# RMS-norm sums in four column tiles with inverses through DRAM, and three moves of work around them, in an attention and convolution kernel

## The chip, the cores and the metric

The kernel runs on one core of one Trainium2 chip. The metric is the device time of one launch in microseconds (us). All arithmetic is in fp32. One profiled execution gives the durations; its span is the time between the first and the last instruction that the profiler records.

## The reference

The input `x` has 4 images of 1024 channels and 32 x 32 positions, so N = 1024 tokens an image. Layer 0 is attention with 16 heads of 64, layer 1 a bottleneck block of convolutions. Cut to what matters:

```python
# layer 0, per image, h = x as tokens (N x 1024)
qkv = h @ w_qkv.T + b_qkv
q, k = apply_rope(q, cos, sin), apply_rope(k, cos, sin)
q, k = rmsnorm(q, q_norm_w), rmsnorm(k, k_norm_w)       # over all 1024 channels of a token
attn = softmax(q @ k.T * hd ** -0.5)                     # per head
out = rmsnorm((attn @ v) @ w_proj.T, norm_out_w) + h     # v * rsqrt(mean(v * v) + eps) * w
# layer 1, on the 4 images together
y = relu(bn(conv1x1(out, w1)))                           # 1024 -> 256 channels, bn over batch and positions
y = relu(bn(conv3x3(y, w2)))                             # 256 -> 256
y = bn(conv1x1(y, w3))                                   # 256 -> 1024
return relu(out + softplus(residual_scale) * y)
```

So each image has three RMS norms (of q, of k, of the output projection y), twelve in all. Each needs, for every token, a sum of squares over 1024 channels and then 1 / sqrt of it.

## The kernel before, in words

**Layout.** Channels lie on the 128 partitions (8 blocks, `NT`), tokens along the free dimension (two halves of `CH` = 512). The four projections Q, K, V and Y (the output projection) of an image are made with block products of the Strassen and Winograd kind: Q, V and Y of images 1 to 3 with two levels (`project2`), the others with one (`project`). The operands of such products are sums and differences of blocks, made by VectorE (L448 to L452 within `project2`), and the products are added up by VectorE (`add`, L466) after ScalarE has copied the first of each out of PSUM (L527 and its neighbours). V is made with tokens on the partitions (`tokens`). Seven outer products make a projection; `outer_done` finishes blocks of the result.

**Order of the work.** The images run one after the other: Q, K, V, attention, Y. TensorE's list is the program's order. Work of other engines is placed among the products by hand: `product_done(share)` is called after products and advances a counter by units (one unit is four fp32 matmuls of 512 columns; TensorE needs 3.45 us for it). `after(n, step)` puts a step n units later, on the list `later`; `waiting` is a queue of steps with costs, of which one is taken whenever the account `room` is positive, and `spend(cost)` charges the account. A cost of `TT` = 0.21 stands for one VectorE operation of 128 x 512. The engines execute their own lists in order, so a VectorE instruction that waits holds up all that is behind it.

**The norms.** While a projection's blocks are finished, ScalarE squares them and VectorE adds the squares over the 8 channel blocks into `total` (128 x 1024; tiles `sqq`, `sqk`, `sqy`). `inverse_rms` then sums over the partitions: for each half one matmul with a 128 x 128 matrix of ones (`ss`, L650), which leaves every partition with the sum; ScalarE takes the root (L651), and a unit later VectorE the reciprocal (L656), 128 x 512 each. The function `then` that comes after differs: for q and k, `rope` multiplies the cosine and sine tables by the inverses (`tables`, L666 and L667), then for each of 8 channel blocks makes two products (`turn`, L673) and adds one into the other, with neighbouring partitions swapped, through two accumulating DMAs on POOL's queue (L679). For y, `o_norm` multiplies y by the inverses (L790), adds the residual x by an accumulating DMA from DRAM (L791) and stores the result to DRAM as `x1d` (L792), both on POOL's queue. It does so for whole channel blocks, but for the last image in 16 halves.

**Attention** goes through 2 token halves `c` and 8 head pairs `hp`. A head pair has 32 matmuls `sc` (L732) for the scores, the exponential on ScalarE (L739), 32 matmuls `cx` (L749) for the product with V, sums of the probabilities on VectorE (`den`, L741 and L743), and a copy of `cx` by ScalarE (L754). After every second pair four matmuls of 32 columns of ones (`dn`, L768) sum the denominators of four heads into four quarters of the partitions of one PSUM bank, and VectorE takes reciprocals (L774), which SP's DMAs spread (L782). `extra` is a list of steps of which one is run in each pair, used by images 0 and 1 only for preparing weights.

**The last image and layer 1.** In the last image's Y, `queue_filters` loads the raw 3x3 filters (nine loads `t_w<-in_w_dram` on SP) and queues five steps in `waiting` that make the sums of the Winograd filters (L857, L859, L860 on VectorE and one multiplication by ScalarE each; three steps on 128 x 512, two on 128 x 1024). The 1x1 convolution (`c`, L809) of images 1 and 2 comes after Y, reading `back`, which SP loads from `x1d`; that of image 3 reads y directly. Batch statistics, the pads (L1013, L1023) and the 3x3 convolution (`c2x`, `c2y`, L1095) follow.

Of the kernel before, what the change touches and what calls it, by code (L numbers as in the profile page):

```python
# [11 lines left out]
F32 = mybir.dt.float32  # L12
# [6 lines left out]
P = 128  # L19
# [66 lines left out]
def program(ctx, tc, x, wblk, w2, w3, vecs, cos, sin, out, bad):  # L86
# [59 lines left out]

    wd2 = dram.tile([3, len(OUTER), len(SUMS), P, CH], F32, name=f"wd2{u}")
    dens = dram.tile([P, CH], F32, name=f"dens{u}")


    with tc.tile_pool(name=f"st{u}", bufs=2) as st, ExitStack() as s:
# [37 lines left out]
        def bank(kind, name):  # L189
            pool, shape = psum[kind]  # L190
            return pool.tile(shape, F32, tag=kind, name=name)

        def temp(name):
            return tmp.tile([P, CH], F32, tag="tmp", name=name)
# [42 lines left out]

        TT = 0.21
        later, waiting = [], deque()
        pace = {"at": 0, "room": 0.0}  # L240

        def spend(cost):
            pace["room"] -= cost
# [1 line left out]
        def after(n, step):  # L245
            later.append((pace["at"] + n, step))

        def product_done(share=1.0):
            pace["at"] += share
            pace["room"] = min(pace["room"] + share, 1.2)  # L250
            due = [s for at, s in later if at <= pace["at"]]
            later[:] = [(at, s) for at, s in later if at > pace["at"]]
            for step in due:
                step()
            while waiting and pace["room"] > 0:
                next_waiting()

        def next_waiting():
# [154 lines left out]
        def project2(b, which, base, right, room, spare, dest, tokens, tag, ready):  # L413
# [97 lines left out]
            second(0)  # L511
            for k in range(len(OUTER)):
                more = k + 1 < len(OUTER)
                o = banks_[k][0]
                mm(o, w[k][2], t_[k][1], False, False)
                nc.scalar.copy(part(k, 0, 1), o)
                product_done(H2)
                ob = banks_[k][2] = bank2("o2", f"p5_{n}_{k}")
                mm(ob, w[k][3], t_[k][0], True, False)
                p5 = temp(f"p5_{n}_{k}").rearrange("p (q e) -> p q e", q=2)  # L520
                nc.scalar.copy(p5, ob)
                product_done(H2)
                if more:
                    start(k + 1)
                    inner(k + 1, 0)
                mm(o, w[k][4], t_[k][2], False, False)
                nc.scalar.copy(part(k, 1, 1), o)  # L527
                after(2 * H2, lambda k=k, p5=p5: add_to(k, 1, 1, p5))
                product_done(H2)
                if more:  # L530
                    second(k + 1)
                    inner(k + 1, 1)
                mm(ob, w[k][5], b_(k, 1, 1), False, True)
                after(2 * H2, lambda k=k, ob=ob: add_to(k, 0, 1, ob))
                product_done(H2)
                mm(o, w[k][6], t_[k][3], False, True)
                if k > 4:
                    after(2 * H2, lambda k=k, o=o: add(target(k, 1, 0), target(k, 1, 0), o))
                else:
                    nc.scalar.copy(part(k, 1, 0), o)  # L540
                after(2 * H2, lambda k=k: outer_done(k))
                product_done(H2)

        def qk_proj(b, base, bs, ts, bias, dst, tag, w1=None, two=None):

# [94 lines left out]

            return operand(bs, ts), room, spare

        def inverse_rms(total, eps, scale, name, then, lag=4):

            def root():
                for c in range(NCH):
                    o = bank("o2", f"ss_{name}_{c}")
                    nc.tensor.matmul(o, ones, total[:, half[c]], start=True, stop=True)  # L650
                    nc.scalar.activation(total[:, half[c]], o, AF.Sqrt, bias=eps, scale=scale)  # L651
                after(1, invert)

            def invert():
                for c in range(NCH):
                    waiting.append((5 * TT, lambda c=c: nc.vector.reciprocal(total[:, half[c]], total[:, half[c]])))  # L656
                    then(c)

            after(lag, root)

        def rope(b, dst, total, eps, scale, w, tag, rc, biased=True):

            def tables():
                nc.vector.tensor_tensor(rc, cosT, total, ALU.mult)  # L666
                nc.vector.tensor_tensor(total, sinT, total, ALU.mult)  # L667

            def turn(f):
                k, other = dst[:, f, :], big_temp(f"{tag}s_{b}_{f}")  # L670
                for i, (t, table) in enumerate(((other, total), (k, rc))):
                    if w is not None:
                        nc.vector.scalar_tensor_tensor(t, k, w[i][:, f : f + 1], table, ALU.mult, ALU.mult)  # L673
                    elif biased:
                        nc.vector.tensor_tensor(t, k, table, ALU.mult)
                    else:
                        nc.vector.scalar_tensor_tensor(t, k, col("bq", f), table, ALU.add, ALU.mult)
                for i in range(2):
                    nc.gpsimd.dma_start(dst[i::2, f, :], other[1 - i :: 2, :], accum_op=ALU.add)  # L679

            def then(c):
                if c == 0:
                    return
                waiting.append((4 * TT, tables))
                for f in range(NT):
                    waiting.append((4 * TT, lambda f=f: turn(f)))

            inverse_rms(total, eps, scale, f"{tag}_{b}", then)
# [93 lines left out]
                    nc.sync.dma_start(w[j * QH : (j + 1) * QH, half[i]], r[q, :])  # L782
                ready.append((c, hp - 1 + i, w[:, half[i]]))

        def o_norm(b, total, ys, last):


            def norm(f, at):
                y = ys[:, f, at]
                nc.vector.scalar_tensor_tensor(y, y, col("ow", f), total[:, at], ALU.mult, ALU.mult)  # L790
                nc.gpsimd.dma_start(y, x[b, f * P : (f + 1) * P, at], accum_op=ALU.add)  # L791
                nc.gpsimd.dma_start(x1d[f, :, b * N + at.start : b * N + at.stop], y)  # L792

            def then(c):
                if last:
                    waiting.extend([(TT, lambda f=f: norm(f, half[c])) for f in range(NT)])
                elif c == 1:
                    waiting.extend([(2 * TT, lambda f=f: norm(f, slice(0, N))) for f in range(NT)])

            inverse_rms(total, eps_rms, 1.0 / C, f"y_{b}", then, 5 if last else 4)  # L800

        def conv1_weights(name):
            return [[block(W1, f, ih, f"c1_{name}_{f}_{ih}") for ih in range(2)] for f in range(NPT)]
# [38 lines left out]

        uw = {}

        def queue_filters():
            raw = t_tiles("w2")
            taps = w2.rearrange("p (c k f) -> p c k f", c=NPT, k=9)
            for dy in range(3):
                for dx, slot in enumerate((0, 1, 3)):
                    nc.sync.dma_start(  # L850
                        raw[dy][:, slot, :].rearrange("p (c f) -> p c f", c=NPT), taps[:, :, 3 * dy + dx, :]
                    )
            two = [tp.tile([P, 2, CH], F32, tag=n, name=f"u2_{n}") for n in ("cos", "sin")]

            def sums_of(g0, g1, g2, new):

                nc.vector.tensor_tensor(new, g0, g2, ALU.add)  # L857
                nc.scalar.mul(g1, g1, 0.5)
                nc.vector.scalar_tensor_tensor(g1, new, 0.5, g1, ALU.mult, ALU.add)  # L859
                nc.vector.tensor_tensor(new, new, g1, ALU.subtract)  # L860

            for dy in range(3):
                r = raw[dy]
                waiting.append((3 * TT, lambda r=r: sums_of(r[:, 0], r[:, 1], r[:, 3], r[:, 2])))
            for h in range(2):
                js = slice(2 * h, 2 * h + 2)
                waiting.append(
                    (6 * TT, lambda h=h, js=js: sums_of(*(raw[dy][:, js] for dy in range(3)), two[h]))
                )
            for i in range(4):  # L870
                for j in range(4):
                    uw[i, j] = two[j // 2][:, j % 2] if i == 2 else raw[(0, 1, None, 2)[i]][:, j]

        def read_back(b, rows=range(NT)):
            for i in rows:
# [29 lines left out]
        for b in range(B):  # L905
# [31 lines left out]
                    made.append(prepare(*todo.pop(0), pieces))  # L937

            extra = [extra_step] * (len(todo) + 1) if todo else []
            late, ready = [], []  # L940
            probs_ = xp.tile([P, N // P, 2, CH], F32, tag="x", name=f"p_{b}")
            for c in range(NCH):
# [34 lines left out]
                        after(5 * (k - 3) + 0.5, lambda k=k: after(4, prepare(1, WV, k, big_pieces)))  # L977
            else:
                back = {B - 3: x_tile(b + 1)}
                after(3, queue_filters)  # L980
                for i in range(NT):
                    after(8 + 1.5 * i, lambda i=i: read_back(B - 3, (i,)))
            yt[b] = kp.tile([P, NT, N], F32, tag="k", name=f"y_{b}")
            two = (2, *in_place(q_all, tc_, yt[b], False)) if b > 0 else None
            ty = qk_proj(b, WP, q_all, tc_, None, yt[b], "y", None, two)
            o_norm(b, ty, yt[b], b == B - 1)

        back[B - 2] = kv.tile([P, NT, N], F32, tag="q", name="back")
        read_back(B - 2)
        w = conv1_weights("last")  # L990
        for b in (B - 3, B - 2):
            for c in range(NCH):
                for f in range(NPT):
                    conv1(b, f, c, w, back[b])
# [335 lines left out]
```

## Time and profile before

| | |
|---|---|
| time, median of 3 runs | 2788.1 us (2787.07 to 2788.9) |
| profiled execution, its own time | 2789.47 us |
| its span | 2787.7 us |
| mean granted TensorE clock | 0.994 |
| TensorE busy | 2741.8 us, 98% of the span |
| VectorE busy | 2001.5 us, 72% |
| ScalarE busy | 1040.6 us, 37% |
| POOL busy | 375.7 us, 13% |
| gaps over 0.5 us in TensorE's list | 30.4 us together |

Engines are written PE (TensorE), DVE (VectorE), ACT (ScalarE), POOL and SP, the last two mostly issuing DMAs. A line of the timeline has the start and the length in us, engine, line, operation, output and inputs by the tiles' names, shapes and the number of instructions run together; in square brackets the idle time of the engine before it and what it waited for. PE shows two records for each fp32 matmul. Busy time is an average over stages: what a change is worth is read at the place where it acts.

### The profile page before, as it was taken

Reading aid. Unit: us, or ns where it says so; the run is one execution under the profiler, and the core shown is the slowest. Engines: PE = TensorE matmul, PEld = TensorE weight load, DVE = VectorE, ACT = ScalarE, POOL = GpSimd, SP = SyncE. Lnnn points to the kernel's source line nnn. Section 1 sums busy time; section 2 is a strip of 40 time slices with the busy share of each in tenths; the row PEclk is TensorE's granted clock in tenths of the full one; section 3 lists DMA queues with packets and bytes.
Section 4 is the critical chain, followed back from the end, with each engine's and each line's share of the span. In section 5 each row is a group of like instructions: output and inputs, shape, how many; then the busy total and the mean of one; then the engine's idle time right before and its main releaser. Section 6 shows DMA issues by size and latency. Waiting matters only on the chain.

```text
span 2787.7 us, 31160 instructions
## 1 busy us (share of the span) xinstructions
PE 2741.8 (98%) x11194; PEld 1568.1 (56%) x11194; DVE 2001.5 (72%) x2209; ACT 1040.6 (37%) x1419; POOL 375.7 (13%) x427
## 2 busy tenths in 40 slices
PE   9999999999999999999999999999999999998997
PEld 4449533348647533488558333687476333855853
DVE  4356599767727898888748777887567777855987
ACT  1221455323222455433322555333223554322266
POOL 1022022121100121101101001101101001011000
PEclk9999999999999999999999999999999999999999
DMA  5366254277645551267647100558555101664165
GB/s 204 98 170 163 85 165 141 82 257 209 178 111 156 141 160 55 58 204 227 160 126 191 35 17 16 166 148 260 136 152 151 24 16 43 188 203 126 62 213 210
DMA packets 211171, 383.90 MB, mean 138 GB/s; under 512 B 24369, under 2 KB 96561, under 8 KB 211009
## 3 DMA queue, kind: packets, MB, share of 16 engines
q1 hardware_dynamic: 178400, 275.85, 31.7%
q0 software_dynamic: 32608, 105.97, 15.7%
q8 instruction: 91, 1.49, 0.2%
q14 instruction: 72, 0.58, 0.1%
HBM read 254.59 MB, written 76.81 MB: 119 GB/s over the span
## 4 chain that ended last, share of the span: by engine, by line
PE 93%; DMA 3%; DVE 2%; ACT 1%; issue 0%; POOL 0%; SPq 0%; DVEq 0%; ACTq 0%; POOLq 0%
PE sc L732 16%; PE cx L749 16%; PE p_v L434 9%; PE p_q L439 8%; PE p_y L439 8%; PE pa_k L295 8%; PE pc_k L295 4%; PE c L1234 4%; PE c L809 2%; PE pa_q L295 2%; PE pa_v L303 2%; PE pa_y L295 2%; PE pb_k L295 2%; PE c2x L1095 2%; PE c2y L1095 2%; DMA y<-in_x_dram 1%
## 5 line engine op out<-in xcount | busy, mean ns | idle before, releaser
L743 DVE TENSOR_TENSOR den<-den,p 128x1024 f32<-128x1024 f32 x384 | 470.5, 1225 | 41.1 <-DVE den L741 0.5
L739 ACT ACTIVATE p<-sc 128x1024 f32<-128x1024 f32 x512 | 476.6, 1043 | 59.9 <-PE sc L732 59.9
L732 PE MATMUL sc<-q,k 64*128 64x512 f32 x2048 | 460.9, 600 | 8.8 <-DVE v L466 7.4
L749 PE MATMUL cx<-p,v 128*64 128x512 f32 x2048 | 453.6, 595 | 0.0
L732 PEld LDWEIGHTS sc<-q,k 64*128 64x128 f32 x2048 | 192.3, 187 | 275.2 <-issue 125.0
L749 PEld LDWEIGHTS cx<-p,v 128*64 128x64 f32 x2048 | 141.4, 137 | 304.3 <-issue 304.3
L713 POOL TENSOR_SCALAR q<-q,vec 128x512 f32<-128x512 f32 x64 | 123.6, 1939 | 676.8 <-DVE q L712 676.8
L754 ACT COPY q<-cx 128x512 f32<-128x512 f32 x64 | 37.5, 586 | 357.5 <-PE cx L749 357.5
L439 PE MATMUL p_y<-q,w_y 128*128 128x256 f32 x696 | 159.3, 383 | 4.1 <-DVE q L449 4.1
L741 DVE TENSOR_TENSOR den<-p 128x1024 f32<-128x1024 f32 x64 | 76.6, 1196 | 120.1 <-ACT p L739 120.1
L434 PE MATMUL p_v<-w_v,x 128*128 128x256 f32 x696 | 157.1, 379 | 0.0
L439 PE MATMUL p_q<-to,w_q 128*128 128x256 f32 x672 | 152.3, 380 | 0.0
L439 PEld LDWEIGHTS p_y<-q,w_y 128*128 128x128 f32 x696 | 132.9, 192 | 25.7 <-DVE q L449 5.0
L434 PEld LDWEIGHTS p_v<-w_v,x 128*128 128x128 f32 x696 | 132.2, 190 | 19.3 <-issue 1.4
L439 PEld LDWEIGHTS p_q<-to,w_q 128*128 128x128 f32 x672 | 128.0, 191 | 19.1 <-issue 1.8
L774 DVE RECIPROCAL rec<-dn 128x512 f32<-128x512 f32 x32 | 107.3, 3354 | 35.8 <-PE dn L768 35.6
L679 POOL DMA_DIRECT2D k<-ks x64 | 55.1, 1017 | 416.2 <-ACT v L499 148.6
L1234 PE MATMUL c<-h,w 128*128 128x512 f32 x256 | 110.3, 592 | 0.9 <-ACT h L1138 0.9
L791 POOL DMA_DIRECT2D y<-in_x_dram x40 | 36.4, 1128 | 352.5 <-DVE y L790 248.8
L1234 PEld LDWEIGHTS c<-h,w 128*128 128x128 f32 x256 | 48.6, 190 | 62.1 <-issue 54.3
L563 DVE TENSOR_TENSOR sqk<-sqk,sq_k 128x512 f32<-128x512 f32 x56 | 37.9, 689 | 62.7 <-ACT sq_k L559 61.4
L679 POOL DMA_DIRECT2D q<-qs x64 | 55.1, 1002 | 183.3 <-ACT sq_k L559 86.6
(527 smaller groups left out, 4176.1 us busy)
## 6 DMA issues: line engine op xcount, KB each, us to landing
w_q<-wd2f SPq DMA_DIRECT2D x84, 256.0 KB
w_v<-wd2f SPq DMA_DIRECT2D x84, 256.0 KB
w_y<-wd2f SPq DMA_DIRECT2D x84, 256.0 KB
wd2f<-w_pre POOLq DMA_DIRECT2D x68, 256.0 KB, 2.8
x<-in_x_dram SPq DMA_DIRECT2D x64, 256.0 KB
q<-qs POOLq DMA_DIRECT2D x64, 256.0 KB, 5.1
k<-ks POOLq DMA_DIRECT2D x64, 256.0 KB, 4.5
inv<-rec SPq DMA_DIRECT2D x256, 64.0 KB
```

The source lines that it names most:

```text
L295: nc.tensor.matmul(o, w[:, i, :], r(i), start=first and i == 0, stop=last and i == NH - 1, skip_group_check=True,)
L434: nc.tensor.matmul(o[:, q].rearrange("p (g f) -> p g f", g=2), r[:, i, q * P : (q + 1) * P], wt[:, :, i, :], skip_group_check=True, **at,)
L439: nc.tensor.matmul(o[:, q], wt[:, q, i, :], r[:, i, :], skip_group_check=True, **at)
L679: nc.gpsimd.dma_start(dst[i::2, f, :], other[1 - i :: 2, :], accum_op=ALU.add)
L713: nc.gpsimd.tensor_scalar(cx, cx, col("bv", hp), None, ALU.add)
L732: nc.tensor.matmul(sc[:, j], k_all[d, hp, t * P : (t + 1) * P], q_all[d, hp, at], start=True, stop=bad is not None,)
L739: nc.scalar.activation(p, sc, AF.Exp)
L743: nc.vector.tensor_tensor(d_, d_, p, ALU.add)
L749: nc.tensor.matmul(o[j * HD : (j + 1) * HD, :], v[:, t, h0 : h0 + HD], probs[t][:, j], start=(t == 0), stop=(t == N // P - 1),)
L774: nc.vector.reciprocal(r, dn)
L1095: nc.tensor.matmul(o[:, r * TR * TC : (r + 1) * TR * TC], uw[2 * h + r, j][:, i * PL + f * P : i * PL + (f + 1) * P], vt[b, i][:, 2 * h + ...
L1234: nc.tensor.matmul(os[i], w3t[k][f // NH][:, f % NH, :], h2[b, k][:, half[c]], start=(k == 0), stop=(k == NPT - 1),)
```

## The change

1. `inverse_rms`: instead of two matmuls with 128 columns of ones, four with 32 columns, each on a quarter of the tokens (256) and into a quarter of the partitions of one bank. One root and one reciprocal of 128 x 256 follow, in a small tile `r`. Then one row of each quarter goes to DRAM (`inv_d`, 4 KB) and is read back spread over all partitions into `total` (512 KB), both on POOL's queue. `then` comes 2.5 units after the reciprocal. The lag before the sums is 4 units for all (5 for the last before).
2. `project2` with tokens, which is V of images 1 to 3: during the last outer product nothing is taken from `waiting` (`hold`), and V's remaining `later` steps are run right after the last product.
3. The filters' sums become five steps of `extra` in the last image's attention, one in each of the head pairs 0 to 4 of the first half, in place of steps in `waiting` during Y.
4. The last image's norm is a function of its own, `last_norm`: VectorE multiplies by the inverses and adds the residual `xr`, which SP loads (8 x 512 KB) into the room of V, and SP stores to `x1d`.

```diff
+    inv_d = dram.tile([3 * B, N], F32, name=f"inv_d{u}")
+    norms_done = list(range(3 * B))
...
-            while waiting and pace["room"] > 0:
+            while waiting and pace["room"] > 0 and not pace["hold"]:
                 next_waiting()
...
             for k in range(len(OUTER)):
                 more = k + 1 < len(OUTER)
+                pace["hold"] = tokens and not more
...
+            if tokens:
+                while later:
+                    product_done(H2)
+            pace["hold"] = False
...
-        def inverse_rms(total, eps, scale, name, then, lag=4):
+        def inverse_rms(total, eps, scale, name, then):
+            r = temp(f"rms_{name}")[:, :QT]
+            row = inv_d[norms_done.pop(0)]
             def root():
-                for c in range(NCH):
-                    o = bank("o2", f"ss_{name}_{c}")
-                    nc.tensor.matmul(o, ones, total[:, half[c]], start=True, stop=True)
-                    nc.scalar.activation(total[:, half[c]], o, AF.Sqrt, bias=eps, scale=scale)
-                after(1, invert)
+                o = bank("o2", f"ss_{name}")[:, :QT]
+                for q in range(4):
+                    nc.tensor.matmul(
+                        o[q * QH : (q + 1) * QH, :], ones[:, :QH], total[:, q * QT : (q + 1) * QT],
+                        start=True, stop=True,
+                    )
+                nc.scalar.activation(r, o, AF.Sqrt, bias=eps, scale=scale)
+                after(0.5, invert)
             def invert():
-                for c in range(NCH):
-                    waiting.append((5 * TT, lambda c=c: nc.vector.reciprocal(total[:, half[c]], total[:, half[c]])))
-                    then(c)
-            after(lag, root)
+                spend(3 * TT)
+                nc.vector.reciprocal(r, r)
+                nc.gpsimd.dma_start(row.rearrange("(q t) -> q t", q=4), r[::QH, :])
+                nc.gpsimd.dma_start(total, row.partition_broadcast(P))
+                after(2.5, then)
+            after(4, root)
...
-                nc.gpsimd.dma_start(y, x[b, f * P : (f + 1) * P, at], accum_op=ALU.add)
-                nc.gpsimd.dma_start(x1d[f, :, b * N + at.start : b * N + at.stop], y)
+                nc.vector.tensor_tensor(y, y, xr[:, f, at], ALU.add)
+                nc.sync.dma_start(x1d[f, :, b * N + at.start : b * N + at.stop], y)
+            def then():
+                waiting.extend([(2 * TT, lambda f=f, at=at: norm(f, at)) for at in half for f in range(NT)])
...
-                waiting.append((3 * TT, lambda r=r: sums_of(r[:, 0], r[:, 1], r[:, 3], r[:, 2])))
+                steps.append(lambda r=r: sums_of(r[:, 0], r[:, 1], r[:, 3], r[:, 2]))
...
             extra = [extra_step] * (len(todo) + 1) if todo else []
+            if b == B - 1:
+                extra = filters()
...
-                after(3, queue_filters)
...
-            o_norm(b, ty, yt[b], b == B - 1)
+            if b + 1 < B:
+                o_norm(b, ty, yt[b])
+            else:
+                xr = v_room("xr")
+                last_norm(b, ty, yt[b], xr)
...
+        for i in range(NT):
+            nc.sync.dma_start(xr[:, i, :], x[B - 1, i * P : (i + 1) * P, :])
```

More of the change, by code (lines that the diff above doesn't have):

```diff
@@ L239, in program @@
         later, waiting = [], deque()
-        pace = {"at": 0, "room": 0.0}
+        pace = {"at": 0, "room": 0.0, "hold": False}
         def spend(cost):
@@ L679, in turn @@
                     nc.gpsimd.dma_start(dst[i::2, f, :], other[1 - i :: 2, :], accum_op=ALU.add)
-            def then(c):
-                if c == 0:
-                    return
+            def then():
                 waiting.append((4 * TT, tables))
@@ L783, in inverses, with o_norm, norm, then @@
                 ready.append((c, hp - 1 + i, w[:, half[i]]))
-        def o_norm(b, total, ys, last):
+        def o_norm(b, total, ys):
+            def norm(f):
+                y = ys[:, f, :]
+                nc.vector.scalar_tensor_tensor(y, y, col("ow", f), total, ALU.mult, ALU.mult)
+                nc.gpsimd.dma_start(y, x[b, f * P : (f + 1) * P, :], accum_op=ALU.add)
+                nc.gpsimd.dma_start(x1d[f, :, b * N : (b + 1) * N], y)
+            def then():
+                waiting.extend([(2 * TT, lambda f=f: norm(f)) for f in range(NT)])
+            inverse_rms(total, eps_rms, 1.0 / C, f"y_{b}", then)
+        def last_norm(b, total, ys, xr):
             def norm(f, at):
@@ L790, in norm, with then @@
                 nc.vector.scalar_tensor_tensor(y, y, col("ow", f), total[:, at], ALU.mult, ALU.mult)
-                nc.gpsimd.dma_start(y, x[b, f * P : (f + 1) * P, at], accum_op=ALU.add)
-                nc.gpsimd.dma_start(x1d[f, :, b * N + at.start : b * N + at.stop], y)
[L794 to L800, printed above, removed]
+                nc.vector.tensor_tensor(y, y, xr[:, f, at], ALU.add)
+                nc.sync.dma_start(x1d[f, :, b * N + at.start : b * N + at.stop], y)
+            def then():
+                waiting.extend([(2 * TT, lambda f=f, at=at: norm(f, at)) for at in half for f in range(NT)])
+            inverse_rms(total, eps_rms, 1.0 / C, f"y_{b}", then)
         def conv1_weights(name):
@@ L843, in program, with filters @@
         uw = {}
-        def queue_filters():
+        def filters():
+            steps = []
             raw = t_tiles("w2")
@@ L863, in queue_filters @@
                 r = raw[dy]
-                waiting.append((3 * TT, lambda r=r: sums_of(r[:, 0], r[:, 1], r[:, 3], r[:, 2])))
+                steps.append(lambda r=r: sums_of(r[:, 0], r[:, 1], r[:, 3], r[:, 2]))
             for h in range(2):
                 js = slice(2 * h, 2 * h + 2)
-                waiting.append(
-                    (6 * TT, lambda h=h, js=js: sums_of(*(raw[dy][:, js] for dy in range(3)), two[h]))
-                )
+                steps.append(lambda h=h, js=js: sums_of(*(raw[dy][:, js] for dy in range(3)), two[h]))
             for i in range(4):
@@ L872, in queue_filters @@
                     uw[i, j] = two[j // 2][:, j % 2] if i == 2 else raw[(0, 1, None, 2)[i]][:, j]
+            return steps
         def read_back(b, rows=range(NT)):
```

## The prediction

> **What bounds the kernel.** I read the busy shares and the chain first. The chain is the work that ended last, followed back; its first line gives shares of the span by engine.
>
> ```profile
> PE 2741.8 (98%) x11194; PEld 1568.1 (56%) x11194; DVE 2001.5 (72%) x2209; ACT 1040.6 (37%) x1419; POOL 375.7 (13%) x427
> PE 93%; DMA 3%; DVE 2%; ACT 1%; issue 0%; POOL 0%; SPq 0%; DVEq 0%; ACTq 0%; POOLq 0%
> ```
>
> TensorE (PE) is the bound: a change pays only by making PE's own list shorter, or by closing one of its gaps. So I went through PE's timeline (start, length, line, idle before, releaser) for every gap over 0.5 us. They sum to 30.4 us: 5.03 at the start, and the rest at some twelve places. The ones this change touches:
>
> ```profile
> 2128.61 8.83 PE L732 MATMUL sc<-q,k 64*128 64x512 f32 x32 [3.11 <-DVE v L466]
> 2144.40 7.14 PE L732 MATMUL sc<-q,k 64*128 64x512 f32 x32
> ...
> 2395.67 7.13 PE L439 MATMUL p_y<-q,w_y 128*128 128x256 f32 x24 [4.14 <-DVE q L449]
> ...
> 2524.50 1.12 PE L809 MATMUL c<-y,w_c_last 128*128 128x512 f32 x2 [2.94 <-DMA y<-in_x_dram]
> 2527.34 19.27 PE L809 MATMUL c<-y,w_c_last 128*128 128x512 f32 x38 [1.72 <-DMA y<-in_x_dram]
> ```
>
> The reader is to see two things. A gap has a named releaser; and the work after a long gap is itself slow: the first 32 `sc` take 8.83 us, the next 7.14. The same holds after the 4.14 us gap (24 products take 7.13, elsewhere 5.34: +1.79) and after the last two (38 at 0.4315 would be 16.4; they take 19.27: +2.9). Image 2 has the same V gap (3.12) and slow start (8.81 against 7.07), image 1 gaps of 1.19 and 0.66 without much of one.
>
> Now the sums of squares, and a product of the shape that the change makes of them:
>
> ```profile
> 2052.83 1.88 PE L650 MATMUL ss_k<-sqk,ones 128*128 128x512 f32 x4
> 2054.55 5.34 PE L434 MATMUL p_v<-w_v,v 128*128 128x256 f32 x24
> ...
> 2158.48 1.07 PE L768 MATMUL dn<-den,ones 128*32 128x512 f32 x8
> 2159.48 2.85 PE L732 MATMUL sc<-q,k 64*128 64x512 f32 x12
> ```
>
> From start to next start, `ss` holds PE 1.72 us (four records of 0.43, two for each fp32 matmul). `dn`, four matmuls of 32 columns into four quarters of a bank, holds it 1.00 us for eight records, which in series would be 3.45.
>
> **The Trainium skill.** "TensorE: Matmul & The Clock Gate", section "What's actually happening": after an idle window of about 3.4 us the array runs at half clock until about 3.4 us of work have passed, with windows that don't align to the program. The trace agrees: gaps of 2.9 to 4.1 us are followed by 1.75 to 2.9 us lost, gaps near 1 us by about 0.4. "TensorEngine Tiling (Array Packing)", section "Available Configurations": in 128x32 mode the array is four independent tiles. The `dn` row agrees: 1.00 us is one matmul (0.863) and 0.13. "DMA: Bandwidth & Descriptors", section "Anatomy of one DMA — SWDGE (gpsimd) path": about 2.0 us fixed, mostly the write receipt, and bytes over 436 GB/s. It gives 2.6 us for 256 KB; `wd2f<-w_pre` lands in 2.8, but `x1df<-y` (512 KB) takes 5.9 against 3.2.
>
> **Part 1, the norms (12 of them).** Removed from each on PE: two full matmuls, 1.72 us. Added: four of 32 columns and 256 elements side by side: half of 0.863 and the same 0.13, 0.56 us. Bounds: 0.43 (no switching cost) and 1.00 (as a whole `dn`), 1.72 if they run in series. `ss` stands back to back on PE in all 12, so 12 x (1.72 - 0.56) = **13.9 us** (15.5; 8.6; 0).
>
> On VectorE (DVE) two reciprocals go and one of half their width comes:
>
> ```profile
> 2054.61 6.56 DVE L656 RECIPROCAL sqk<-sqk 128x512 f32<-128x512 f32 x2 [0.89 <-ACT sqk L651]
> 2061.21 1.22 DVE L666 TENSOR_TENSOR rk<-cosT,sqk 128x1024 f32<-128x1024 f32 x1
> ```
>
> 6.56 becomes about 1.7 us. That frees DVE where PE doesn't wait: nothing. ScalarE's two roots of 0.69 become one of about 0.45: nothing, hidden under PE.
>
> The new wait is the way through DRAM: root 0.6, reciprocal 1.7, issue of the 4 KB store 0.6 to 1, store 2.0 (by the page; up to 5.1, the median landing of `q<-qs`), issue of the broadcast 1.0, broadcast of 512 KB 3.2 (by the page; up to 7.9, the slowest row of that size). That is 9 to 17 us after `ss`; I take 10, as most norms fall where few transfers run. The tables (L666) or the norm's products (L790) are released 0.5 and 2.5 units after it, a unit being four fp32 products of 512 columns, 3.45 us: 10.4 us. So DVE meets the broadcast about when it lands. If it comes late, DVE stands still in order, with the projection's adds and operand differences behind it, and PE behind those. But before, DVE was held there for 6.56 us by the reciprocals and PE's list shows no gap; that is the tolerance: 10.4 + 6.6 = 17 us. Cost zero up to there; beyond, 12 us for each microsecond. On POOL two DMA issues a norm (about 2 us of a queue that is 13% busy) stand ahead of the swaps (L679), which have microseconds to spare.
>
> **Part 2, the end of V.** In the last outer product the turns of K (L673) no longer get between V's last adds:
>
> ```profile
> 2124.04 1.28 DVE L673 SCALAR_TENSOR_TENSOR ks<-k,wqk_other,sqk 128x1024 f32<-128x1024 f32 x1
> 2125.36 1.28 DVE L673 SCALAR_TENSOR_TENSOR k<-k,wqk,rk 128x1024 f32<-128x1024 f32 x1
> 2126.56 0.68 DVE L466 TENSOR_TENSOR x<-x,p_v 128x512 f32<-128x512 f32 x1
> 2127.27 0.69 DVE L466 TENSOR_TENSOR v<-v,x 128x512 f32<-128x512 f32 x1
> 2127.88 0.68 DVE L466 TENSOR_TENSOR v<-v,p_v 128x512 f32<-128x512 f32 x1
> ```
>
> V's last product ends on PE at 2125.50; the last add starts 2.4 us later because two turns (2.6 us) stood ahead. Without them it starts at once: gap 0.68 and about 0.17 to wake, 0.85. Images 2 and 3: 3.12 - 0.85 = 2.27 and the slow start of 1.75, 4.0 each; image 1: 1.85 of gaps. Together **9.9 us**. The deferred turns (three, 7.7 us) now run beside the first heads; K's later features aren't needed for some 14 us a head, and the first `den` sums start 0.6 us later: nothing.
>
> **Part 3, the filter sums.** In the last output projection L857 to L860 hold DVE from 2388.35 to 2394.2, just ahead of q (L448, L449), for which PE waits. Moved away: 4.14 + 1.79 = **5.9 us**. In the last attention DVE is busy some 177 of 238 us and ScalarE, whose exponentials need 7.4 of 14.6 us a head, is idle 0.5 to 1.5 us at the copies behind which the added products (0.6 or 1.1 us) go. Five steps of 2 to 3.7 us on DVE: the first four fit; the last delays one `dn` by about half a microsecond. Cost 0.75 (0 to 3). The nine loads of raw filters (256 KB each, on SP) are already issued at 2079 to 2126, ahead of that attention, so the earlier sums wait for none of them. Net **5.2 us**.
>
> **Part 4, the last residual.** 16 accumulating DMAs of 256 KB (7.7 us to land) and 16 stores leave POOL; DVE gets 16 pairs of 0.69. The inverses are complete about 11 us after `ss` (at 2481 on the old clock), the first half of y at about 2496, the second at 2508. With its gaps closed PE wants them at 2510 and 2517. The residual's rows, eight loads of 512 KB by SP into V's old room beside those of `back`, land about 2476; the stores on SP and the pads' memset on POOL (needed 2529) have room. Gaps 2.94 + 1.72 and slow start 2.9: **7.6 us**.
>
> **Sum.** 13.9 + 9.9 + 5.2 + 7.6 = 36.5 us. The profiled execution took 2789.5 (span 2787.7, about 1.8 around it), so 2753.0; it stood 1.4 over the median of 2788.1. Forecast: **2751.6 us**, span about 2751. Waits for weights (`w_q<-wdf`: 1.98 and 1.41, the first with 1.9 of slow start) fall beside the y norms' traffic, which changes; they may go or grow, ±3.
>
> **Rivals.**
> - The four matmuls run in series, or the mode switch eats what they save. For: they alternate with full-array products. Against: `dn` does the same. Part 1 is then 0: 2765.5.
> - Gaps close only partly: PE still starts slowly (1.79 + 2 x 1.75 + 2.9 = 8.2 lost) or the last rows still come late (7.6 lost). For: the windows aren't aligned, and the tail hangs on three transfers in a row. Against: 9 us of slack. About 2760.
> - Slower: the inverses come late, because the store's and the broadcast's issue stand on POOL behind swaps that wait. Each L679 issue takes 1.0 us; eight ahead make a way of 10 us into 18, ten make it 20. From 17 us on, PE pays twelve times; at 20 us the 36.5 are cancelled, at 22 us it is 12 x 5 - 36.5 = +23.5: 2811.6. Against: POOL is 87% idle, and the former norm's swaps are issued long before.
> - The slower way in part, near 20 us: no change.
>
> **Chances.** Forecast 0.62, columns in series 0.12, gaps partly 0.20, inverses late 0.04, late by just as much 0.02. A measurement of this kernel tells about 0.2%, 5.6 us, from no change. Faster 0.94, same 0.02, slower 0.04. The range takes the upper bounds (15.5 for Part 1, 2 more at the V ends, 3 at the weights) at its low end, 2743, and the first two rivals with an attention cost of 2 to 3 us at its high end, 2768.
>
> **What would show it.** Right: `ss` rows of 0.5 to 0.6 us; no gap at 2.5 us or more but those for weights, the start and `c2x`; first `sc` near 7.1 us; one `c` run at the end without a DMA releaser. Wrong: `ss` at 1.7 us from start to start; gaps on PE released by DVE tables or y soon after each norm; DVE idle for over 6 us ahead of the tables or the norm's products, with the broadcast as releaser.

## The result, and the profile after

The changed kernel takes 2771.61 us (median of 6 runs, 2769.1 to 2774.17) against 2785.35 us before (6 runs): a ratio of 0.9951, 95% interval 0.9938 to 0.9963, 13.7 us less. The forecast was 36.5 us less. The direction was right, the size was not, and the time lies above the forecast's range.

The profiled execution took 2769.1 us, the lowest of the six; its span of 2767.3 us is 20.4 us under the span of before, more than the medians differ. PE's timeline in the changed kernel (start, length, line, shapes, idle before, releaser) at the places that the forecast named:

```profile
2051.94 0.64 PE L660 MATMUL ss_k<-sqk,ones 128*32 128x256 f32 x8
2052.51 5.45 PE L436 MATMUL p_v<-w_v,v 128*128 128x256 f32 x24
...
2124.35 7.14 PE L745 MATMUL sc<-q,k 64*128 64x512 f32 x32 [0.78 <-DVE v L468]
...
2385.99 5.34 PE L441 MATMUL p_y<-q,w_y 128*128 128x256 f32 x24
...
2498.67 27.63 PE L833 MATMUL c<-y,w_c_last 128*128 128x512 f32 x64
```

`ss` holds PE 0.57 us from start to start; the V gap is 0.78 and the first `sc` take 7.14; no gap of 4.14 us is left in the last output projection; the last convolution runs through. All this is as forecast. What is not as forecast is in the middle of Q, at images 1, 2 and 3:

```profile
680.63 3.78 PE L441 MATMUL p_q<-t,w_q 128*128 128x256 f32 x8 [3.99 <-DMA w_q<-wdf]
684.21 3.20 PE L441 MATMUL p_q<-to,w_q 128*128 128x256 f32 x8
...
1301.68 3.45 PE L441 MATMUL p_q<-t,w_q 128*128 128x256 f32 x8 [3.97 <-DMA w_q<-wdf]
1304.97 1.89 PE L441 MATMUL p_q<-to,w_q 128*128 128x256 f32 x8
...
1316.71 1.99 PE L441 MATMUL p_q<-x,w_q 128*128 128x256 f32 x8 [1.22 <-DMA w_q<-wdf]
...
1896.63 3.78 PE L441 MATMUL p_q<-t,w_q 128*128 128x256 f32 x8 [4.72 <-DMA w_q<-wdf]
1900.21 2.78 PE L441 MATMUL p_q<-to,w_q 128*128 128x256 f32 x8
```

In the kernel before, PE waits for `w_q` at three places:

```profile
680.19 1.99 PE L439 MATMUL p_q<-t,w_q 128*128 128x256 f32 x8 [0.94 <-DMA w_q<-wdf]
...
1313.77 3.36 PE L439 MATMUL p_q<-x,w_q 128*128 128x256 f32 x8 [1.98 <-DMA w_q<-wdf]
...
1911.39 1.99 PE L439 MATMUL p_q<-x,w_q 128*128 128x256 f32 x8 [1.41 <-DMA w_q<-wdf]
```

Gaps with `w_q` as releaser add up to 13.9 us, where before had 0.94 + 1.98 + 1.41 = 4.3; after three of them eight records take 3.45 to 3.78 us instead of 1.89. From Q's first product to the first of the next stage, images 1 to 3 take 92.90 + 92.55 + 92.99 = 278.4 us against 87.89 + 90.26 + 88.36 = 266.5, although each holds a shorter `ss_y`, which saves 0.95 us (worked out below). So the weights cost 11.9 + 2.9 = 14.8 us more than before.

What may make the weights late shows in POOL's timeline at image 2, first of the changed kernel, then of the kernel before:

```profile
1280.09 0.91 POOL L804 DMA_DIRECT2D y<-in_x_dram  x1 [6.05 <-DVE y L803]
1281.27 0.86 POOL L804 DMA_DIRECT2D y<-in_x_dram  x1 [0.27 <-issue]
1282.45 0.86 POOL L804 DMA_DIRECT2D y<-in_x_dram  x1 [0.32 <-issue]
1287.47 0.56 POOL L805 DMA_DIRECT2D x1df<-y  x1 [4.16 <-DMA y<-in_x_dram]
1290.69 0.56 POOL L805 DMA_DIRECT2D x1df<-y  x1 [2.66 <-DMA y<-in_x_dram]
1293.96 0.53 POOL L805 DMA_DIRECT2D x1df<-y  x1 [2.71 <-DMA y<-in_x_dram]
```

```profile
1278.70 0.94 POOL L791 DMA_DIRECT2D y<-in_x_dram  x1 [91.64 <-DVE y L790]
1282.09 0.89 POOL L791 DMA_DIRECT2D y<-in_x_dram  x1 [2.46 <-issue]
1286.14 0.56 POOL L792 DMA_DIRECT2D x1df<-y  x1 [3.16 <-DMA y<-in_x_dram]
1290.17 0.54 POOL L792 DMA_DIRECT2D x1df<-y  x1 [3.47 <-DMA y<-in_x_dram]
```

Three residual transfers of 512 KB now start within 2.4 us, and three stores behind them; before it was two and two. What has changed ahead of them is on DVE, again first in the changed kernel and then in the kernel before: the reader is to see the `x3`.

```profile
1278.26 3.67 DVE L803 SCALAR_TENSOR_TENSOR y<-y,vec,sqy 128x1024 f32<-128x1024 f32 x3
```

```profile
1276.85 1.28 DVE L790 SCALAR_TENSOR_TENSOR y<-y,vec,sqy 128x1024 f32<-128x1024 f32 x1
...
1280.25 1.28 DVE L790 SCALAR_TENSOR_TENSOR y<-y,vec,sqy 128x1024 f32<-128x1024 f32 x1
...
1290.17 1.28 DVE L790 SCALAR_TENSOR_TENSOR y<-y,vec,sqy 128x1024 f32<-128x1024 f32 x1
```

Before, the two reciprocals were taken from `waiting` at 5 `TT` each, so the account was in debt when the norm's products came up, and they were let through singly. Now the reciprocal costs 3 `TT`, 2.5 units pass until the products are queued, the account fills to its cap of 1.2, and three products at 2 `TT` (0.42) go at once. In the program each product is followed by its residual and its store; in the trace POOL issues three residuals and then three stores, so the order of its list is not that of the program's text. The DMA engines' share and rate (the two last columns) in stretches of 5 us, by the table of stretches of the changed kernel:

```profile
1285.00:1290.00 5.00, 5.00 (x25) 4.38 (x25) 4.96 (x7) 4.04 (x7) 0.56 (x1) 1.00 1.06 233
1290.00:1295.00 5.00, 5.00 (x25) 4.41 (x24) 4.89 (x8) 0.59 (x1) 1.60 (x3) 1.00 1.03 318
1295.00:1300.00 5.00, 2.71 (x13) 2.05 (x11) 4.96 (x6) 1.17 (x2) 0.41 (x1) 1.00 1.08 394
```

The DMA engines are full for 15 us (a transfer's packets count where they start, so a share can pass 1), and in the third stretch PE is busy for only 2.71 of the 5 us (the number after the comma).

### The profile page after: what moved, and what is told of

It is laid out like the page before. It is cut to its first block, busy times and chain, and to the rows that moved or that the text cites. A ratio compares the mean times of both kernels' runs of the same rounds, so it can differ in the third digit from the quotient of the medians.

```text
span 2767.3 us, 31322 instructions
## 1 busy us (share of the span) xinstructions
PE 2727.7 (99%) x11242; PEld 1561.1 (56%) x11242; DVE 1955.9 (71%) x2213; ACT 1029.5 (37%) x1407; POOL 368.9 (13%) x419
## 4 chain that ended last, share of the span: by engine, by line
PE 97%; DMA 2%; DVE 1%; ACT 0%; issue 0%; SPq 0%; ACTq 0%
PE sc L745 16%; PE cx L762 16%; PE p_v L436 9%; PE p_y L441 9%; PE p_q L441 9%; PE pa_k L297 8%; PE c L833 4%; PE pc_k L297 4%; PE c L1266 4%; PE pa_q L297 2%; PE pa_v L305 2%; PE pb_k L297 2%; PE pa_y L297 2%; PE c2x L1127 2%; PE c2y L1127 2%; DMA w_q<-wdf 1%
## 5 line engine op out<-in xcount | busy, mean ns | idle before, releaser
L316 ACT COPY k<-pa_k 128x512 f32<-128x512 f32 x48 | 28.1, 586 | 116.3 <-PE pa_k L297 116.3
L571 DVE TENSOR_TENSOR sqq<-sqq,sq_q 128x512 f32<-128x512 f32 x56 | 38.4, 690 | 44.5 <-ACT sq_q L567 42.0
```

## The experiments

Theory A: the row of three y products, and so of three residual transfers, holds up Q's weights. Rival B: the new broadcasts do. Rival C: the waits vary by the run. Each group of runs had runs of the kernel before beside it, with medians of 2785.9 to 2787.8 us, so the medians below are set against each other directly, to 1 or 2 us; ratios are to before. The gaps are those of one profiled execution of each kernel, whose own time can lie some us from the median (e5's took 2787.25 us, e10's 2753.99).

| kernel | median, us | ratio, interval | `w_q` gaps in its profile, us |
|---|---|---|---|
| changed kernel again | 2772.35 | 0.9941 (0.9928 to 0.9955) | 19 |
| e1, products one at a time | 2749.82 | 0.9864 (0.9849 to 0.9879) | 1.2 |
| e2, norms only | 2786.19 | 0.9991 (0.9984 to 0.9998) | 18 |
| e3, parts 2 to 4 only | 2769.24 | 0.9929 (0.9915 to 0.9943) | 3.8 |
| e4, no residual transfers | 2748.97 | 0.9856 (0.9841 to 0.9871) | none |
| e5, e3 with the products in a row | 2782.61 | 0.9980 (0.9973 to 0.9987) | 17 |
| e6, e1 without part 2 | 2749.16 | 0.9858 (0.9843 to 0.9873) | none |
| e7, e1 with full columns | 2759.84 | 0.9898 (0.9883 to 0.9913) | 0.6 |
| e8, e1 with two in a row | 2755.58 | 0.9892 (0.9873 to 0.9911) | 6.8 |
| e9, e1 without part 3 | 2754.69 | 0.9882 (0.9866 to 0.9899) | 2.2 |
| e10, e1 without part 4 | 2757.52 | 0.9897 (0.9880 to 0.9913) | none |
| e11, e2 one at a time | 2762.26 | 0.9916 (0.9901 to 0.9931) | 0.5 |

**e1, one at a time.** One line in `o_norm`, which puts the account back into debt:

```diff
             def then():
+                spend(3 * TT)
                 waiting.extend([(2 * TT, lambda f=f: norm(f)) for f in range(NT)])
```

> The changed kernel, with the y norms of images 0 to 2 charged three more VectorE operations before their products, so that VectorE makes the first three products of a norm one at a time among the projection's adds, as before the change, and not three in a row. Theory A (bunching: the residual reads and stores of three channel blocks start together and take the DMA engines from the weights of Q, for which PE waits): the w_q waits fall from 13.9 us to 4 to 6, their slow starts with them; 8 to 13 us less than the changed kernel, so 22 to 27 us under the kernel before. Theory B (the twelve new broadcasts of 512 KB take the DMA engines): waits stay near 14 us, 14 us under before. Theory C (the waits vary from run to run whatever the kernel): no steady difference to the changed kernel beyond 3 us.

e1 is 22 us under the changed kernel and 37.4 under the one before. The direction is A's; the size is well beyond the 8 to 13 and 22 to 27 us that were expected. The waits fell not to the 4 to 6 us expected but to 1.2, below the 4.3 of before: the expectation took one at a time for the order of before, which POOL's timeline has as two and two. The first product stands where it stood, 10.7 us after the start of `ss_y` in both kernels, so it is the spacing that changed. e1's POOL timeline at image 2 has one transfer, one store, in turn:

```profile
1272.69 0.91 POOL L804 DMA_DIRECT2D y<-in_x_dram  x1 [6.08 <-issue]
1279.97 0.56 POOL L805 DMA_DIRECT2D x1df<-y  x1 [6.37 <-DMA y<-in_x_dram]
1280.51 0.90 POOL L804 DMA_DIRECT2D y<-in_x_dram  x1
1288.86 0.56 POOL L805 DMA_DIRECT2D x1df<-y  x1 [7.45 <-DMA y<-in_x_dram]
```

POOL issues in order, so each store's wait for its residual holds back the next residual: POOL's own list limits the traffic as long as the order is one and one. At this place e1 is 7.4 us earlier than the changed kernel (`ss_y` starts at 1260.12 instead of 1267.52), so the stretches that match, to half a microsecond, are:

```profile
1278.00:1283.00 5.00, 5.00 (x25) 4.40 (x24) 2.86 (x4) 4.04 (x7) 1.44 (x2) 1.00 0.92 305
1283.00:1288.00 5.00, 5.00 (x25) 4.38 (x24) 4.86 (x9) 0.59 (x1) 0.00 (x0) 1.00 0.99 220
1288.00:1293.00 5.00, 5.00 (x25) 4.41 (x24) 5.00 (x5) 1.76 (x3) 1.45 (x2) 1.00 1.02 318
```

The DMA engines are nearly as full here, and PE doesn't stop. The first two stores now land 4.8 and 4.3 us after their issue; in the changed kernel the three took 8.0, 7.4 and 6.6. The broadcasts are all still there, so B falls.

**The changed kernel again**, unaltered:

> The changed kernel itself, unaltered, on the same chip as the kernels beside it. Theory A (three products of y in a row start three residual transfers together, which hold up Q's weights): about -14 us against before, w_q waits near 14 us in every profile and slow starts of 5 us after them, so 18 to 24 us over the version that makes the products one at a time. Theory C (the waits vary by the run): a time that may lie anywhere between -14 and -36.

The time is 2772.35 us, and the profile has the long waits at the same places (6.36, 5.71, 4.86) and two short ones (1.11, 1.04). By the stages of Q, as above, the weights cost 18.8 us more than before here, where the first profile had 14.8. So the waits vary by some us, but C, which would have them come and go, falls.

**e2, norms only:** the new `inverse_rms` and `then` put into the kernel before.

> The kernel before with the new norms alone (part 1 for all twelve norms; V's end, filter sums and last residual as before, the last norm's sums 4 units late instead of 5). On PE the sums save 12 x 1.05 = 12.6 us (1.15 less each, and 0.09 lost ahead of each). Theories A and B: the w_q waits come with it, about 10 us of gaps and 5 of slow starts: 0 to +4 us against before. Theory C and the recorded forecast: -12 us or so.

e2 is 1 us under before by the medians. On PE it saves 11.4 us at the sums and, as e6 shows below, some 10 us at the end of V. The waits for weights, with 18 us of gaps and the slow records after them, eat most of that.

**e3, parts 2 to 4 only:** `inverse_rms` as before in the changed kernel.

> The changed kernel with the norms as before (two full matmuls, two roots and two reciprocals of 128x512, no way through DRAM): parts 2, 3 and 4 alone. By the stages of the two traces these gave 9.9 + 5.3 + 7.8 = 23 us. Theories A and B: the w_q waits are those of before, about 4 us of gaps, so -21 to -24 us against before, that is faster than the whole change. Theory C: waits anywhere from 4 to 14 us, -13 to -23.

e3 is 18 us under before, 3 short of the range, with `w_q` gaps of 3.8 us, as before's 4.3. The missing 3 us are in the attention: that of images 1 to 3 takes 234.4 + 233.6 + 236.4 us, 3.7 more than in the changed kernel. At image 3, where four deferred turns stand ahead of the first `den` and not three, PE waits for it:

```profile
2149.97 1.05 PE L774 MATMUL dn<-den,ones 128*32 128x512 f32 x4 [1.41 <-DVE den L749]
```

Part 1 and the rest are thus worth -1 and -18 us apart, and -14 to -15 together.

**e4, no residual transfers:**

```diff
                 nc.vector.scalar_tensor_tensor(y, y, col("ow", f), total, ALU.mult, ALU.mult)
-                nc.gpsimd.dma_start(y, x[b, f * P : (f + 1) * P, :], accum_op=ALU.add)
```

> The changed kernel without the accumulating DMAs that add the residual to y for images 0 to 2 (8 x 512 KB each; the residual of these images is left out of the result). Theory A: with nothing but the stores left to collide with, the w_q waits are 0 to 3 us, -25 to -30 us against before. Theory B: the broadcasts are still there, waits above 8 us, about -14 to -18.

e4 is 38 us under its group's median of before (2787.2), with no gap for weights: more than A expected, although the products still stand in a row of three. The row hurts by its transfers, not by DVE's time. The stores of the first three blocks are in a row here too (issued at 1273.20, 1274.39 and 1275.82), so stores alone don't do it: the residual transfers are needed. e1 gets within 1 us of e4 and adds the residual.

**e5, the row without a broadcast:** e3 with this in `invert`, and `invert` half a unit after the sums:

```diff
-                for c in range(NCH):
-                    waiting.append((5 * TT, lambda c=c: nc.vector.reciprocal(total[:, half[c]], total[:, half[c]])))
-                then()
+                spend(3 * TT)
+                for c in range(NCH):
+                    nc.vector.reciprocal(total[:, half[c]], total[:, half[c]])
+                after(2.5, then)
```

> Parts 2 to 4 with the norms as before on PE and ScalarE and with two reciprocals of 128x512, but with these charged 3 VectorE operations at once and the products released 2.5 units later, as in the changed kernel: the first three y products of a norm then stand in a row although there is no way through DRAM and no broadcast. The same kernel with the reciprocals charged as before gave -18 us. Theory A: the row of three is enough: w_q waits of 10 us or more and their slow starts, 12 to 18 us slower than that, 0 to -6 us against before. Theory B (the broadcasts are needed for it): no broadcast, no change, about -18 us.

e5 is 13.4 us slower than e3, with 17 us of `w_q` gaps, by the release alone. So the row is enough, with the old norms and no broadcast.

**e8, two in a row:** `spend(2 * TT)` in place of 3.

> The version with the y products one at a time, charged 2 VectorE operations instead of 3 ahead of them: POOL's list then has two residual transfers, two stores, as the first two have it in the kernel before, instead of one of each in turn (e1) or three and three (the changed kernel). Theory A by the number of transfers that run together: w_q waits between those of e1 (1.2 us) and of the changed kernel (14 to 18 us), near the 4.3 us of before: 3 to 9 us slower than e1. If any row is as bad as three: 20 us slower. If only the charge's total matters: as e1 within 2 us.

e8 is 5.8 us over e1, with 6.8 us of gaps: the cost grows with the number of residual transfers at the head of a norm that run together. With one the profiles have gaps of 0 to 2.2 us (e1, e6, e7, e9, e10, e11), with two 3.8 to 6.9 (before, e3, e8), with three 14 to 19 (the changed kernel twice, e2, e5).

**e6, without part 2:** e1 without `hold` and without the loop over `later`.

> The version with the y products one at a time, without part 2 (turns of K may again stand between V's last adds). The recorded forecast: the gaps of 3.1 us at images 2 and 3 come back with their slow starts, and 1.85 us at image 1: 8 to 10 us slower than with it. Rival: with the new norms alone the profile had gaps of 0.78 us there, since the turns no longer fall behind V's end when the reciprocals are gone: no difference beyond 1.5 us, so part 2 adds nothing where part 1 is made.

e6 shows no difference to e1. DVE's timeline of e6 at the end of V of image 3:

```profile
2095.63 1.29 DVE L683 SCALAR_TENSOR_TENSOR k<-k,wqk,rk 128x1024 f32<-128x1024 f32 x1
2098.88 0.69 DVE L468 TENSOR_TENSOR x<-x,p_v 128x512 f32<-128x512 f32 x1 [1.97 <-ACT x L530]
2099.61 0.69 DVE L468 TENSOR_TENSOR v<-v,x 128x512 f32<-128x512 f32 x1
2100.22 0.68 DVE L468 TENSOR_TENSOR x<-x,p_v 128x512 f32<-128x512 f32 x1
2100.93 0.69 DVE L468 TENSOR_TENSOR v<-v,x 128x512 f32<-128x512 f32 x1
2101.72 0.69 DVE L468 TENSOR_TENSOR v<-v,p_v 128x512 f32<-128x512 f32 x1
2102.32 1.28 DVE L683 SCALAR_TENSOR_TENSOR ks<-k,wqk_other,sqk 128x1024 f32<-128x1024 f32 x1
```

With the shorter norms the turns fall elsewhere, and none stands between the last adds. The same gap of 0.78 us is in e3 (part 2 alone) and in e2 (part 1 alone): either closes it.

**e7, full columns:** two `ss` matmuls of 128 columns over 512, and four roots of 32x256 out of their banks.

> The version with the y products one at a time, with the sums by two matmuls of 128 columns and 512 elements as before (and the roots taken from the quarters of their two banks in four operations of 32x256); all else, the way through DRAM too, unchanged. If PE's time for the sums is what part 1 brings: 12 x 1.05 = 12.6 us slower. Rival (it came mostly from the freed VectorE and not from PE): under 5 us slower.

e7 is 10.0 us slower than e1, and 10.7 slower than e6, which ran beside it: it is PE's time, not DVE's. The expected 12.6 us counted 1.05 for each sum; by the two profiles it is 0.95, 11.4 in all. Of these e1 gives back about 0.9 us, by which it loses more than e7 in the stages of Q.

**e9, without part 3**, and **e10, without part 4**, each from e1:

> The version with the y products one at a time, without part 3: the filter sums are queued during the last image's output projection again. By the forecast's own sum 5.2 us slower than with it (4.14 gap + 1.79 slow start - 0.75 in attention). Rival: with DVE freed of the reciprocals the queue has drained by then and PE waits less, 0 to 3 us.

> The version with the y products one at a time, without part 4: the last image's residual by 16 accumulating DMAs and 16 stores on POOL. By the forecast's own sum 7.6 us slower than with it (gaps 2.94 + 1.72, slow start 2.9). Rival: the inverses are complete 5 to 6 us earlier than before, so that the chain of transfers ends earlier and only a part of the gaps returns, 2 to 5 us.

They are 4.9 and 7.7 us slower than e1. e9's profile has gaps of 0.84 and 3.05 in the last output projection; e10's has one of 4.70 with the residual's transfer as releaser.

**e11:** e2 with `spend(3 * TT)` ahead of the y products of images 0 to 2.

> Part 1 alone on the kernel before, as in the run of the norms only, with the y products of images 0 to 2 charged 3 VectorE operations ahead, so that they come one at a time. Theory A and additive parts: the version with all parts (37.4 us under before) less part 3 (4.9) and part 4 (7.7) and nothing for part 2: -23 to -26 us against before, that is over 20 us faster than the norms alone. If the parts are not additive, or the rest of the run of the norms only came from something other than the row of three: -10 us or less.

e11 is 23.7 us under before. The parts are additive once the row is gone: 2749.8 + 4.9 + 7.7 = 2762.4, measured 2762.3, closer than these medians can tell (e10's four runs span 6.8 us).

## Why the prediction was wrong

- **The step that failed** is in Part 1: "That frees DVE where PE doesn't wait: nothing." The two reciprocals were more than DVE time. Their charge of 10 `TT` also metered the y products that followed. With them gone these come in a row, and so do the transfers they release. The sum carried the waits for weights at ±3; they were +14.8 in the first profile and +18.8 in the second. The forecast priced each DMA that the change adds, and not the start times of DMAs that it leaves alone. That three products come in a row follows from the charges in the program and needed no run to be seen. That POOL then issues three residuals ahead of the first store does not stand in the program's text; only a trace shows it, and why the order comes out so is not shown. That the row is the cause is shown by e1 and e5, its residual transfers as the carrier by e4. Whether residuals in a row would do it without the stores was not tried.
- **The sums on PE**: forecast 0.56 us each, measured 0.57; the group ahead of them takes about 0.09 longer (16 records to the next start 3.55 against 3.46), and the group behind 0.10 to 0.11 (24 records 5.28 against 5.18), which the sum left out. From 24 records ahead to 40 behind, each of the twelve saves 0.95: 11.4 us instead of 13.9. The rival of matmuls in series is out.
- **The end of V**: forecast 9.9. From V's first product to the output projection's, images 1 to 3 gained 3.46 + 4.95 + 4.39 = 12.8 us, of which 2.9 are the shorter `ss_k`: 9.9, with the filter sums' 0.6 us in the last attention (233.9 us, and 233.3 in e11 without them) already taken off. The size was right, the owner wrong: e6 and e2 show that Part 1 gives it alone, so in this change Part 2 is worth nothing. Nor are its deferred turns free, as the prediction had them, where the old norms stand beside them: e3.
- **Filter sums**: forecast 5.2, e9 4.9 by the medians, and 5.5 by PE's stages (the last output projection is 6.1 us longer than in e1, the last attention 0.6 shorter). **Last residual**: forecast 7.6, e10 7.7 by the medians, and 7.8 by the stage of the last convolution.
- **The way through DRAM**: forecast 10 us, tolerance 17. For K of image 3 the sums start at 2051.94 and the tables at 2062.68, 10.7 us, with no DMA as releaser; in none of the twelve norms does DVE wait for the broadcast. The rival of late inverses did not happen. The 3.2 us for the broadcast, from the Trainium skill's "DMA: Bandwidth & Descriptors", section "Anatomy of one DMA — SWDGE (gpsimd) path", was low: the twelve broadcasts land in 4.0 to 4.8.
- **Slow starts** went with the gaps that closed (the first `sc` take 7.14 us and not 8.83) and came after the new ones of 4 to 5 us, as the Trainium skill's "TensorE: Matmul & The Clock Gate", section "What's actually happening", led to expect. Its idle window of about 3.4 us is no limit here: before, a gap of 1.98 us was followed by eight records in 3.36 us instead of 1.89. The gaps of 0.94 and 1.41 were followed by 1.99, only 0.1 more and not the 0.4 that the prediction gives for gaps near 1 us.
- e1 is 1.8 us under the forecast time, and part of that is luck. In its Q stages 5.6 us of waits for weights are gone that the kernel before had, more than the ±3 of the forecast, while the sums bring 2.5 us less than forecast. The sizes of the other parts were sound; the one collision missing from the sum was worth 22 us.
- The low end of the range is 2 us off its own terms (2751.6 - 1.6 - 2 - 3 = 2745, not 2743); nothing hangs on it.

## What to carry to other kernels

When an edit frees an engine off the critical path, ask what that engine's work was metering: list the DMAs that its later instructions release, and compare their order and spacing before and after, not only the number of them. Spread bulk transfers that nobody awaits at once, so that a stream of loads beside them, each needed soon after it is issued, comes in time; here one charged line (22 us) was worth more than the change itself (14 us). When two edits cure one stall, only an experiment with one of them tells which of them is paid for it.

## What the runs showed that I had not expected

- The DMA engines can be at a share of 0.92 to 1.02 for 15 us without a stall (e1), while 1.03 to 1.08 at the same place stop PE (the changed kernel). The rate doesn't tell the two apart either: e8 has 406 GB/s at a share of 1.05 with PE busy throughout (1286.3 to 1291.3), and the stretch with the stall has 394. What differs in the traces is how many bulk transfers are issued together, and how long they take to land.
- A wait of 4 to 5 us costs 40 to 80% as much again in slow records: after gaps of 3.99 and 4.72 us the first eight records take 3.78 us each time instead of 1.89, and the next eight still 3.20 and 2.78: 3.2 and 2.8 us lost behind the gaps. After the gap of 3.97 only the first eight are slow (3.45): 1.6 us lost.
